# A two-layer gated block with routed experts: one group's results stored by block and fetched by token, the last two blocks added by matrix products, and a new order

## The chip, the cores and the metric

The kernel runs on one core of a Trainium2 chip. Its engines work beside each other, each through its own list of instructions in order: TensorE (PE: matrix products; PEld is its weight load), VectorE (DVE), ScalarE (ACT), GpSimd (POOL) and SyncE (SP, which only issues transfers here). They are held together by semaphores. Transfers between the chip's memory and the on-chip buffers run on 16 DMA engines, issued by SP, ACT or POOL. The metric is the device time of one execution in microseconds; less is better.

## The reference

The input x is 4 batches of 512 tokens of 128 numbers. Two layers follow each other; each is an attention over 77 context rows and a mixture of experts:

```python
x = x + tanh(g_xattn[l]) * attention_l(layernorm(x), ctx)      # 16 heads of 8
x = x + tanh(g_ffn[l])   * experts_l(layernorm(x))             # top 2 of 8 experts
# experts: softmax over 8 logits, the best two; each h = gelu(x @ w1[e] + b1[e]) (512 wide),
#          y = h @ w2[e] + b2[e]; the token gets p1 * y1 + p2 * y2
```

The second layer's attention adds a bias by position and a mask. All is float32.

## The kernel before, in words

**Attention.** A batch keeps its 512 tokens as 4 tiles of 128. Per layer and batch the steps are: statistics (`LS`), normalisation on ACT (`LT`), transposes (`LU`), query (`Q`), four score groups whose maxima DVE takes (`S`), lowering the query by the maxima (`M`, `W`), four exponent groups on PE and ACT (`X`), their sums with the values (`U`), the ratio (`E`, `T`, `N`) and the output product added to x (`F`). In layer 2 `S` and `X` also multiply a turned copy of the mask, tile `mt` (line 833, two buffers), into the products. The copy is made by `mask` on POOL, stored to memory, and loaded again by `mturn` (line 835).

**Routing.** The batches form two groups: 0 and 1, 2 and 3. For each token `Routing` finds the best two experts and the token's place in each expert's region of a table in memory, `xgs[group]`. `send` (line 525) gives the row numbers. `scatter` (line 538) sends the normalised rows there with indirect DMAs, one for 128 rows, all from POOL (line 419); each is preceded by a memset of a spare tile (line 418). A row carries 130 numbers: 128 of the token, its probability, and the row where its result belongs. `table` and `registers` turn the counts into 16 blocks a group, 7 of 256 rows and 9 of 128, whose first rows SP reads from registers.

**Experts.** Each block loads its expert's weights (`w`, line 623, 5 buffers) and its rows (`x`, line 631), transposes them (`t`), multiplies up (`u`, line 658; GELU on ACT, line 664), and down (`d`, line 673). DVE then adds the bias, multiplies by the probability (lines 681, 687) and makes the row numbers of the results (line 692). `y` scatters the block's results to `yks[layer][group]`, again by indirect DMAs of 128 rows from POOL. When a group's blocks are all scattered, `CL` loads each token's two results (line 711) and `CA` adds them to x (line 718), on POOL in layer 1, on DVE in layer 2, where the sum is also stored as output.

**Order.** The order of all steps is written out by hand in one long string, `ORDER`, of words such as `0y13.1`: layer 0, step y, block 13, group 1 (for attention and routing the last number is the batch). Every engine and every queue takes its own instructions in the order of these words. PE's matmul results go through six rotating PSUM banks.

Of the kernel before, what the change touches and what calls it, by code (L numbers as in the profile page):

```python
# [39 lines left out]
ROWS = SPARE + 2 * CAP  # L40


@with_exitstack
def flamingo_kernel(ctx: ExitStack, tc: tile.TileContext, a: dict, out: bass.AP):
# [53 lines left out]
    def load_mask(b):  # L98
        t = keep.tile([P, NT * KV + S], I32, tag="mi", name="mi", bufs=2)
        nc.sync.dma_start(out=t, in_=a["masks"][b])  # L100
        msk_i[b] = t
# [307 lines left out]

    class Scatters:  # L410


        def __init__(self):
            self.sent = []

# [11 lines left out]
    class Routing:  # L427


        def __init__(self, l, group):  # L430
            self.l, self.group = l, group
            self.carry = None
            self.left = {}
            self.scatters = Scatters()
# [47 lines left out]
        def choose(self):  # L482

            sm = self.sm
            self.pick = sm("pick", (P, 2, NT, E))
# [40 lines left out]
        def send(self, b):  # L526
# [8 lines left out]
            with nc.allow_low_precision(reason="one whole number and zeros"):  # L535
                nc.vector.tensor_reduce(to, v, AX.X, ALU.add)
            self.left[b] = self.chosen, to

        def scatter(self, b, t):
            rows, to = self.left[b]  # L540
# [3 lines left out]
        def table(self):  # L544
# [41 lines left out]
            nc.vector.scalar_tensor_tensor(hit[:, MARKS // 2 * E :], tail, block_no, row, ALU.is_equal, ALU.mult)  # L586
            begin = sm("begin", (P, 1))
# [13 lines left out]
    class Blocks:  # L601


        def __init__(self, routing):
            self.r, self.l, self.group = routing, routing.l, routing.group
            self.w, self.x, self.xT, self.h, self.y = {}, {}, {}, {}, {}
# [61 lines left out]
        def down(self, i):  # L668
            n, w, h, x = self.size(i), self.w.pop(i), self.h.pop(i), self.x.pop(i)
# [19 lines left out]
            )  # L689

# [3 lines left out]

        def scatter(self, i):
            yb, to = self.y.pop(i)
            for s in range(self.size(i)):
                self.scatters.send(yks[self.l][self.group], yb[:, s, :], to[:, s : s + 1])

    class Combine:  # L700


        def __init__(self, l, b):
            self.l, self.b = l, b

# [9 lines left out]
        def add(self):  # L715
# [3 lines left out]
            if self.l == 1:  # L719
                (nc.scalar if self.b == B - 1 else nc.sync).dma_start(out=out[self.b].rearrange("(p t) d -> p t d", p=P), in_=x)  # L720
# [11 lines left out]
    def routing_constants():  # L732
# [25 lines left out]
        return rank, region, below, ones, upper, mark, nth, block_no, row_of, pair_at, spare  # L758
# [3 lines left out]
    fill = const.tile([P, CAP // P * PAY], F32, tag="fill", name="fill")  # L762
# [4 lines left out]

    def clear(g, q):
        xg = xgs[g]
        for e in range(4 * q, 4 * q + 4, 2):  # L770
            nc.sync.dma_start(
                out=xg[e * REGION : (e + 2) * REGION, :].rearrange("(r q) d -> r (q d)", r=2)[:, : CAP * PAY].rearrange(
                    "r (p f) -> p r f", p=P
                ),
                in_=fill.unsqueeze(1).to_broadcast([P, 2, CAP // P * PAY]),
            )
        if q == 0:
            nc.sync.dma_start(
                out=xg[UNUSED : UNUSED + 256, :].rearrange("(p r) d -> p (r d)", p=P), in_=fill[:, : 2 * PAY]
            )  # L780

# [63 lines left out]
    def part(l, name, n):  # L845
        k, i = name[0], name[1:]
        A, R = at[l][n], routings[l][n // 2]
        if i.isdigit():
            i = int(i)
            if k in "wxtudy":  # L850
                G = blocks[l][n]
                {"w": G.load_w, "x": G.load_x, "t": G.turn, "u": G.up, "d": G.down, "y": G.scatter}[k](i)
            else:
                {"S": A.scores, "X": A.exps, "U": A.sums, "E": A.sums_out, "T": A.ratio, "Z": lambda t: R.scatter(n, t)}[k](i)
        elif name == "RS":
            R.stats(n)
        elif k == "R":
            {"T": R.turn, "U": R.turned, "L": R.logits, "C": R.choose, "D": R.choose_second, "M": R.count, "N": R.places, "X": lambda: R.send(n), "G": R.registers, "B": R.table}[i]()
# [8 lines left out]
        vclear0 pads0 ldx0 ones0 hot1 ldwv ldctx slots hot2 0LS.0 ldo0 ldgates ldq0 vclear2 gate keys0 vclear1 ldx1  # L867
        ldx2 hot5 ones1 ldx3 0LT.0 0LS.1 ldpos ldmask1 values1 0LS.2 values0 hot0 0LU.0 fill values2 second 0Q.0 0LT.1
        0S3.0 0LT.2 hot4 0S2.0 cleara1 0S0.0 cleara0 0LU.1 ldmask0 0LU.2 0S1.0 mask1 0Q.1 0M.0 0W.0 0S3.1 0Q.2 0LS.3
        0S2.1 0X0.0 0S0.1 0X1.0 0S1.1 pads1 0U0.0 0X2.0 0M.1 0U1.0 0E0.0 clearb0 0W.1 0X3.0 routing 0U2.0 0X0.1 0U3.0  # L870
# [132 lines left out]
```

## Time and profile before

| what | value |
|---|---|
| median of 3 runs | 428.34 us (427.59 to 429.42) |
| the profiled execution: its own time | 429.68 us |
| the profiled execution: its span | 427.6 us |
| mean granted PE clock | 0.966 |
| indirect DMAs: layer inputs, results | 64, 92 |
| one indirect DMA on POOL, its memset | 974 ns, 514 ns |
| moved by DMA | 77.91 MB, mean 182 GB/s |

The span runs from the first to the last instruction; the execution's own time has some 2 us around it. The page's second section cuts the span into 40 slices of 10.7 us; a digit is the busy share in tenths, and PEclk the clock that was granted to PE, in tenths. A group line names the line of the program, engine, operation, output and inputs, then how often it ran, busy time in all, the mean in ns, and the idle time before it. A timeline line gives start and length in us, then the instruction, and in brackets how long the engine had stood idle and what ended that. A line that begins with two times and a colon sums a stretch: the busy time of PE, PEld, DVE, ACT and POOL with instruction counts, then the clock, the DMA share and GB/s.

### The profile page before, as it was taken

To read this page: it belongs to the slowest core of one execution; us is meant where nothing else is said; L and a number is where in the kernel's file an instruction comes from. 1 tells how busy PE (TensorE), PEld (TensorE's weight loads), DVE (VectorE), ACT (ScalarE), POOL (GpSimd) and SP (SyncE) were. 2 spreads that over 40 slices of the span, in tenths; PEclk is the share of its full clock that TensorE was granted. 3 is DMA by queue.
4 is the path that set the end of the run, shared out by engine and by line. 5 is a ranking of instruction groups with operands and counts; after the bars stand their busy time and mean duration, and the time that the engine had idled before them with its cause. 6 is when DMAs were issued, how large, how long until landed. Compare 5 with 4: busy or idle time off the path is not lost.

```text
span 427.6 us, 9653 instructions
## 1 busy us (share of the span) xinstructions
PE 385.3 (90%) x3236; PEld 271.4 (63%) x3236; DVE 244.9 (57%) x931; ACT 225.0 (53%) x529; POOL 295.5 (69%) x478
## 2 busy tenths in 40 slices
PE   5999999987899999989999999999889999999850
PEld 2454545433789999987772355442669789988840
DVE  7786768864447634376774379684648233333342
ACT  2556776663374654447455965446564344435430
POOL 4743312887698989869986450987289898989860
PEclk9999999996699999999999999999989999999995
DMA  7396091112956799986514221014743776789855
GB/s 191 158 372 202 3 325 72 33 44 83 317 150 207 224 361 295 313 299 218 167 45 151 80 60 62 26 45 122 236 129 105 272 232 192 266 285 289 269 204 182
DMA packets 38977, 77.91 MB, mean 182 GB/s; under 512 B 6224, under 2 KB 22608, under 8 KB 38928
## 3 DMA queue, kind: packets, MB, share of 16 engines
q1 hardware_dynamic: 32640, 65.66, 47.9%
q0 software_dynamic: 4992, 10.30, 6.7%
q10 hardware_dynamic: 1296, 1.34, 0.9%
q8 instruction: 26, 0.43, 0.4%
q14 instruction: 23, 0.19, 0.1%
HBM read 55.47 MB, written 21.80 MB: 181 GB/s over the span
## 4 chain that ended last, share of the span: by engine, by line
PE 68%; DVE 12%; DMA 6%; POOL 5%; ACT 4%; issue 3%; SPq 0%; DVEq 0%; ACTq 0%; POOLq 0%
PE mm L673 16%; PE mm L658 15%; PE mm L353 8%; PE o L367 7%; PE mm L305 6%; POOL xg L419 3%; PE mm L279 3%; DVE mx L313 2%; PE mm L347 2%; ACT eT L359 2%; POOL apart L418 2%; PE mm L241 2%; PE mm L643 2%; PE mm L406 2%; DMA xb<-xg 1%
## 5 line engine op out<-in xcount | busy, mean ns | idle before, releaser
L664 ACT ACTIVATE h<-mm,w 128x128 f32<-128x128 f32 (+1 forms) x256 | 86.7, 415 | 99.3 <-issue 55.9
L419 POOL DMA_INDIRECT yk<-yb,to x92 | 89.6, 974 | 18.5 <-issue 12.2
L658 PE MATMUL mm<-xbT,w 128*128 128x128 f32 (+1 forms) x512 | 95.0, 331 | 6.6 <-DVE xbT L645 5.5
L673 PE MATMUL mm<-w,h 128*128 128x128 f32 x736 | 96.0, 281 | 0.7 <-ACT h L664 0.4
L673 PEld LDWEIGHTS mm<-w,h 128*128 128x128 f32 x736 | 89.2, 191 | 6.5 <-ACT h L664 3.6
L658 PEld LDWEIGHTS mm<-xbT,w 128*128 128x128 f32 x512 | 77.1, 194 | 15.0 <-DVE xbT L645 7.7
L418 POOL MEMSET apart<- 1x512 f32 x156 | 80.2, 514 | 0.1
L359 ACT ACTIVATE eT<-mm 77x512 f32<-77x512 f32 x128 | 65.4, 592 | 26.2 <-PE mm L353 25.7
L419 POOL DMA_INDIRECT xg<-rows,rows_to x64 | 62.8, 981 | 15.2 <-issue 13.0
L681 DVE TENSOR_TENSOR yb<-mm,w 128x128 f32<-128x128 f32 (+1 forms) x64 | 22.3, 348 | 67.2 <-PE mm L673 58.6
L313 DVE TENSOR_REDUCE mx<-mm 128x4 f32<-128x308 f32 x128 | 52.1, 469 | 11.5 <-PE mm L305 11.3
L353 PE MATMUL mm<-qa,kb 32*77 32x512 f32 x256 | 41.3, 617 | 0.5 <-DVE mx L313 0.5
L222 POOL TENSOR_SCALAR rstd<-mv 128x4 f32<-128x4 f32 x16 | 3.8, 236 | 54.2 <-DVE mv L220 40.9
L645 DVE COPY xbT<-mm 128x128 f32<-128x128 f32 (+1 forms) x64 | 21.7, 344 | 30.4 <-PE mm L643 30.4
L367 PE MATMUL o<-eT,vb 128*32 128x512 f32 x256 | 36.6, 631 | 0.0
L305 PE MATMUL mm<-kb,q 32*128 32x154 f32 x512 | 31.8, 322 | 0.8 <-DVE mx L313 0.5
L305 PEld LDWEIGHTS mm<-kb,q 32*128 32x128 f32 x512 | 22.6, 183 | 12.4 <-issue 3.1
L687 DVE TENSOR_TENSOR yb<-yb,xb 128x128 f32<-128x128 f32 (+1 forms) x64 | 24.1, 376 | 2.2
L643 PE MATMUL mm<-ident,xb 128*128 128x128 f32 x92 | 20.5, 281 | 1.2 <-DMA xb<-xg 1.2
L353 PEld LDWEIGHTS mm<-qa,kb 32*77 32x77 f32 x256 | 10.5, 140 | 13.4 <-issue 5.6
L223 POOL TENSOR_TENSOR rstd<-rstd,mhalf 128x4 f32<-128x4 f32 x16 | 16.7, 1044 | 1.3
L219 DVE BATCH_NORM_STATS2 st<-x 128x6 f32<-128x128 f32 x64 | 17.1, 267 | 0.2
(155 smaller groups left out, 445.6 us busy)
## 6 DMA issues: line engine op xcount, KB each, us to landing
w<-in_experts SPq DMA_DIRECT2D x64, 578.0 KB, 5.0
xg<-fill SPq DMA_DIRECT2D x8, 1040.0 KB, 6.0
xb<-xg SPq DMA_DIRECT2D x28, 130.0 KB, 3.6
y<-yk SPq DMA_DIRECT2D x14, 256.0 KB, 3.9
mt<-turns SPq DMA_DIRECT2D x4, 820.0 KB
xb<-xg SPq DMA_DIRECT2D x36, 65.0 KB, 4.4
mi<-in_masks SPq DMA_DIRECT2D x4, 410.0 KB
turns<-mb SPq DMA_DIRECT2D x8, 205.0 KB
```

The costliest lines, as they stand in the source:

```text
L305: nc.tensor.matmul(view[g][:, h], lhsT=self.q[h][rows, t * P : (t + 1) * P], rhs=kbs[l][rows, h, :, b, :], start=(l == 0), stop=(l == 0 or ...
L313: nc.vector.tensor_reduce(self.mx[:, t, :, 2 * g : 2 * g + 2], view[g], AX.X, ALU.max)
L353: nc.tensor.matmul(ps[g][:KV, :], lhsT=kbs[l][rows, h, w, b, :], rhs=self.qa[h][rows, :], start=(l == 0), stop=True,)
L359: nc.scalar.activation(self.eT[j][g][:KV, :], ps[g][:KV, :], AF.Exp)
L367: nc.tensor.matmul(self.o[a][g * 32 : (g + 1) * 32, :], lhsT=vbs[self.b][:, self.l, g, j, :], rhs=self.eT[j][g], start=(w == 0), stop=(w = ...
L418: nc.gpsimd.memset(apart, 0.0)
L419: i = nc.gpsimd.indirect_dma_start(out=to[:, :], out_offset=bass.IndirectOffsetOnAxis(ap=index, axis=0), in_=rows, in_offset=None)
L643: nc.tensor.transpose(ps[:, s * P : (s + 1) * P], x[:, s, :D], ident)
L658: nc.tensor.matmul(ps[:, g * 256 : g * 256 + n], lhsT=w[:, c * P : (c + 1) * P], rhs=xT[:, :n], start=True, stop=True,)
L664: nc.scalar.activation(h[:, c, :n], ps[:, g * 256 : g * 256 + n], AF.Gelu_apprx_tanh, bias=w[:, B1_AT + c : B1_AT + c + 1])
L673: nc.tensor.matmul(y[:, s * P : (s + 1) * P], lhsT=h[:, c, s * P : (s + 1) * P], rhs=w[:, W2_AT + c * P : W2_AT + (c + 1) * P], start=(c = ...
L687: nc.vector.tensor_tensor(yb[:, :n, :], yb[:, :n, :], x[:, :n, D : D + 1].to_broadcast([P, n, D]), ALU.mult)
```

## The change

1. **First layer, group 1.** A block's results are no longer scattered to their tokens' rows. SP stores each block as it is to a new table `yg`. `results` (new step `RP`, on DVE, per batch) works out in which row of `yg` each token's two results lie; for this `table` leaves three numbers per expert, and `send` keeps its row numbers as floats too. New steps `C0` to `C7` then fetch a batch's results, 128 rows each, by indirect DMAs from POOL, with the same memset ahead of each. They take the place of `CL` for batches 2 and 3.
2. **Second layer, group 1, last two blocks.** They are not scattered. `match` (step `o`) compares each row's target with the 512 token positions of a batch and makes a matrix of ones and zeros for both batches; `give` (called by `y`) multiplies it with the block's results and adds the product to x. `CL` and `CA` of batches 2 and 3 come before the last of these, with rows in memory that were cleared by the new step `cleary`, and the output is stored by `give` of block 15.
3. **Room.** The zero tile `fill` has 4 rows instead of 8 a partition, and clearing takes one DMA an expert instead of one for two; the integer mask `mi` has one buffer instead of two; `pick` has three.
4. **Order.** The whole string is laid out anew. Among much else, the turned masks are loaded for batches 1, 0, 2, 3 instead of 0, 1, 2, 3, and around the end of layer 1 it reads:

```
before: ... 0d12.1 0t15.1 1S2.1 0u14.1 1W.0 1S1.1 0d13.1 0u15.1 0y10.1 0y11.1 1X0.0 0y12.1 0d14.1 0y13.1 0y14.1
        0d15.1 1S3.1 0y15.1 1U0.0 1M.1 0CL.2 1X1.0 1X2.0 1U1.0 1W.1 1X3.0 1E0.0 1U2.0 0CL.3 mask2 0CA.2 1X0.1 1LS.2
        1U3.0 1E1.0 1X1.1 1LT.2 1U0.1 1T0.0 1X2.1 mturn2 1T1.0 1U1.1 1LU.2 0CA.3 1LS.3 1N.0 1X3.1 1F.0 1Q.2 ...
after:  ... 0u14.1 0u15.1 0d14.1 0y13.1 0d15.1 0y15.1 1S0.0 1M.0 0y14.1 0C0.2 0C7.2 1Q.1 0C1.2 1S1.1 1W.0 1S0.1
        0C0.3 1X0.0 1X1.0 1U0.0 1X2.0 0C6.2 1U1.0 1S3.1 1S2.1 ldmask3 0C4.2 0C2.3 0C7.3 0C2.2 1E0.0 1U2.0 0C5.2
        0C3.2 1M.1 1X3.0 0C6.3 1T0.0 1W.1 0C1.3 1X0.1 1U3.0 0C3.3 1E1.0 0CA.2 0C4.3 1LS.2 1X1.1 1T1.0 1U0.1 0C5.3
        1LT.2 1N.0 1X2.1 1LU.2 0CA.3 1F.0 1RS.0 1LS.3 1U1.1 1E0.1 1X3.1 mturn2 1T0.1 1Q.2 1S0.2 1U2.1 ...
```

The end of layer 2 reads in the new order:

```
... 1y12.1 1t14.1 1d13.1 1y13.1 1t15.1 1o14.1 1CL.1 1u14.1 1d14.1 1CA.1 1u15.1 1CL.2 1CL.3 1d15.1 1y14.1 1o15.1 1CA.2 1CA.3 1y15.1
```

The core of the diff:

```diff
+        def fetch(self, to, rows, index):
+            nc.gpsimd.memset(apart, 0.0)
+            nc.gpsimd.indirect_dma_start(
+                out=to, out_offset=None, in_=rows[:, :], in_offset=bass.IndirectOffsetOnAxis(ap=index, axis=0)
+            )
...
+        def results(self, b):
+            for k in range(3):
+                nc.vector.tensor_tensor(v[:, k], pick, self.of[:, k].unsqueeze(1).to_broadcast([P, 2 * NT, E]), ALU.mult)
+            nc.vector.tensor_reduce(r, v, AX.X, ALU.add)
...
+        def match(self, i):
+            for b in range(2):
+                nc.vector.tensor_scalar(oh[:, b], token_at, tok[:, b : b + 1], None, ALU.is_equal)
...
+        def give(self, i):
+            for b in range(2):
+                ps = bank()
+                for t in range(NT):
+                    own = slice(t * P, (t + 1) * P)
+                    nc.tensor.matmul(ps[:, own], lhsT=oh[:, b, own], rhs=yb[:, 0, :], start=True, stop=True)
+                x = x_sb[2 + b]
+                nc.vector.tensor_tensor(x, x, ps.rearrange("p (t d) -> p t d", d=D), ALU.add)
+                if i == NBLK - 1:
+                    (nc.scalar if b else nc.sync).dma_start(out=out[2 + b].rearrange("(p t) d -> p t d", p=P), in_=x)
...
         def scatter(self, i):
+            if self.last(i):
+                self.give(i)
+                return
             yb, to = self.y.pop(i)
+            if to is None:
+                nc.sync.dma_start(
+                    out=yg[self.at(i) : self.at(i) + n * P, :].rearrange("(s p) d -> p s d", p=P), in_=yb[:, :n, :]
+                )
+                return
```

## The prediction

> **What bounds the kernel now.** I read the page's engine and slice rows first, then the busy time by 10 us stretches, then the timeline around the three places that the change touches.
>
> ```profile
> PE 385.3 (90%) x3236; PEld 271.4 (63%) x3236; DVE 244.9 (57%) x931; ACT 225.0 (53%) x529; POOL 295.5 (69%) x478
> PE   5999999987899999989999999999889999999850
> PEclk9999999996699999999999999999989999999995
> L419 POOL DMA_INDIRECT yk<-yb,to x92 | 89.6, 974 | 18.5 <-issue 12.2
> L418 POOL MEMSET apart<- 1x512 f32 x156 | 80.2, 514 | 0.1
> ```
>
> PE is the bound nearly everywhere: 42.3 of 427.6 us idle, about 14 of it at the end. POOL is behind it: each indirect DMA costs 0.974 + 0.514 + a 0.17 gap = 1.64 us.
>
> ```profile
> 100.00:110.00 10.00, 8.07 (x43) 4.58 (x42) 6.11 (x29) 1.29 (x3) 5.95 (x11) 0.67 0.57 159
> 110.00:120.00 10.00, 9.70 (x48) 8.25 (x47) 4.14 (x15) 6.19 (x13) 7.82 (x11) 0.74 0.85 291
> 210.00:220.00 10.00, 10.00 (x145) 7.72 (x144) 8.58 (x26) 3.69 (x11) 8.98 (x14) 1.00 0.13 42
> 250.00:260.00 10.00, 9.07 (x146) 5.80 (x143) 8.78 (x27) 5.21 (x12) 1.78 (x3) 1.00 0.42 131
> ```
>
> Columns: length; busy PE, weight load, DVE, ACT, POOL; granted clock; DMA share; GB/s. From 120 to 250 PE is full (idle 2.5 us in 130), so nothing that only relieves POOL there can shorten the run. From 250 to 300 it idles 2.5 us. In the second layer's experts POOL is gapless too: its row over 311.3 to 410.5 counts 60 indirect DMAs, and 60 x 1.64 = 98.4 of 99.2 us.
>
> The handover of batch 2 to the second layer:
>
> ```profile
> 221.78 2.05 PE L673 MATMUL mm<-w,h 128*128 128x128 f32 x16
> 225.59 0.96 POOL L419 DMA_INDIRECT yk<-yb,to  x1 [0.17 <-issue]
> 230.74 2.63 POOL L718 TENSOR_TENSOR x<-x,y 128x512 f32<-128x512 f32 x2 [1.16 <-DMA y<-yk]
> 235.62 1.04 POOL L223 TENSOR_TENSOR rstd<-rstd,mhalf 128x4 f32<-128x4 f32 x1
> 240.84 1.65 ACT L233 ACTIVATE xn<-x,nmr,rstd 128x128 f32<-128x128 f32 x4
> 243.46 0.66 PE L241 MATMUL mm<-ident,xn 128*128 128x128 f32 x4
> 248.67 0.35 PE L295 MATMUL mm<-mt,ident 32*32 32x308 bf16 x16
> ```
>
> The last expert block leaves PE at 223.83. Batch 2's sum is ready at 233.37, its normalisation could start at 236.9 and starts at 240.84: some 4 us of slack. And the end:
>
> ```profile
> 412.30 1.26 PE L673 MATMUL mm<-w,h 128*128 128x128 f32 x8
> 414.56 1.16 POOL L419 DMA_INDIRECT yk<-yb,to  x1 [0.73 <-DVE to L692]
> 417.11 0.82 ACTq L711 DMA_DIRECT2D y<-yk  x2
> 422.16 2.02 DVE L718 TENSOR_TENSOR x<-x,y 128x512 f32<-128x512 f32 x3 [0.67 <-DMA y<-yk]
> 424.21 0.34 ACTq L720 DMA_DIRECT2D out<-x  x1
> ```
>
> PE ends at 413.56; scatter, load, sums and store take 14.0 us more.
>
> **Part 1, first layer, group 1.** Out: 23 scatters (37.7 us of POOL) and the four loads of batches 2 and 3. In: 16 direct stores on SP and 16 gathers (26.2 us of POOL). While PE is full the relief is worth only the stall that POOL's sums and their DVE slowdown caused at 191.80 (1.1 us). The cost is position: the scatters ran beside the blocks, and a gather can start only when the last block is stored. Call T the end of the last block's matmuls.
> Results written T+0.65 (DVE 0.29 + 0.29 and gaps). Stores issued by T+1.05, landed T+3.6: no row has a direct store of 65 KB alone; between 1.4 (end of the last scatter at 415.72 to the load that it released at 417.11) and 4.4 (median 65 KB load), I take 2.5. Then POOL, in its new order, does 14 gathers before batch 2's sum: 13 x 1.64 + 0.97 = 22.3, to T+25.9. No gather is in the trace; nearest is the scatter of the same 128 rows of 512 B. Its DMA part could be 0.6 to 1.2 us, 14 times; I take the row, 0.97. Sum 2.63: T+28.7. Statistics 1.75, rstd 1.35 (after one more gather, hidden by the statistics), shift 0.2, normalise 1.65, transposes: T+33.9.
> PE arrives at those transposes earlier. Moved behind T are four score groups (1.32 each), a query (1.9), a lowering (0.6) and one exponent group (1.6): 9.4 us, so T falls about 9.4 us earlier. I walked PE, DVE (1.63 per score group) and ACT (2.04 per exponent group) in the new order: PE gets there at T+28.8. Stall 4.5 us.
>
> **Part 2, the turned masks.** The two buffers of mt are now filled for batch 1, then batch 0, so batch 2's copy overwrites batch 1's and must wait for batch 1's last exponents. In the new order only 0.7 us of transposes and 1.9 us of query stand between those and batch 2's first scores. The copy at 235.32 moved data until about 239.6, 4.3 us: stall about 1.8 (nothing if other waits are later, 3 on a busy queue). Queued behind it on PE are the sums that would have filled it. First scores of batch 2: T+42.1. Before, 248.67 is T+24.8 by the old T, T+34.2 by the new, 34.9 with the transposes that now come first: 7.2 us later. PE's idle 2.5 us from 250 to 300 is all that can give it back; I take 1.5.
>
> **The clock.** Idle PE costs twice. After 94.9 PE stood for 2.49 us, then 0.68 twice with little work, and the two rows above lost 10 x (0.33 + 0.26) = 5.9 us of full clock. [...]
>
> **Part 3, the last two blocks.** Out: two scatters and their wait; batches 2 and 3 are loaded after the 60th indirect DMA instead of the 62nd. In, per block: 16 matmuls at 0.112 = 1.8 us of PE, three tiny and two 128x512 comparisons on DVE, two 128x512 sums from PSUM (0.75 each, as at line 408). A comparison is not in the trace: between 0.35 and 0.69 us (the tensor sum of that size), I take 0.5. Two paths. POOL's: last send ends 410.4, lands 411.9, loads 4.4, four sums 2.8, two last sums 1.5, store 3.4 (424.21 to 427.6): 424.0. DVE's: PE end 413.56, second-last block's sums to 416.2, comparisons to 417.8, four sums to 420.6, last two to 422.2, store: 425.6. The one gains 3.6, the other 2.0; I take 2.7.
>
> **Part 4, what is costed at nothing.** DVE: eight 8-column copies (0.17 to 0.3), 16 small operations in the results (about 4 us for both batches) and 5 in the table (1 us), against 18 operations of 0.15 to 0.23 that go; DVE is under 60% busy beside the experts, and 1 us on the path if it is not. The 16 stores wait on SP for a block's product with weight and row loads queued behind; those wait for the same blocks to free their buffers (48.9 us of SP waits), so nothing; uncovered, 1 to 2 us of PE per late weight. Clears: 18 DMAs instead of 10, and a new 1 MB one, some 0.45 us of SP each, ahead of masks and batch 3's rows, which are not needed until 30 us. One mask input buffer: each load waits for the POOL pass before it, early enough in the order. New order of the start: x of batch 0 meets as many DVE memsets, and its normalisation waited for ACT's key copies to 11.77 anyway: 0, give or take 1. The stretch of 88 to 110: output product moved ahead of a sum, its ACT copy uncovered instead: 0, give or take 2. The experts' order in layer 2: POOL still has 60 sends in a row, so 0, give or take 2.
>
> **Sum.** +7.2 +1.7 -1.5 -1.1 -2.7 = +3.6 us. The profiled execution's span is 427.6 and its own time 429.68, 2.1 around it and 1.3 above the median of the runs; applied to the median 428.34 this gives 431.9.
>
> **Rivals.**
> *Gathers hidden (faster).* If batch 2's sum is ready by T+23.8, PE never waits at its transposes. It decides at a gather of 1.29 us with its memset (a DMA part of 0.62) or if PE needs 34 us rather than 29 for the stretch without losing them elsewhere. Then -1.1 and -2.7 stand alone: 424.5. For: the new order puts three of batch 3's gathers ahead of batch 2's sum, which makes sense only where there is slack, and relieving POOL is real. Against: 1.64 us has held in 156 of 156 indirect DMAs.
> *Even.* The stalls come, but at full clock, with all 2.5 given back and the tail at 3.6: 428.34 + 7.2 - 1.1 - 2.5 - 3.6 = 428.3.
> *Clock falls as at 97 (slower still).* 5.9 instead of 1.7 and the tail at 2.0: 428.34 + 7.2 + 5.9 - 1.5 - 1.1 - 2.0 = 436.8.
>
> **Numbers.** About 0.5% (2.1 us) is what a measurement of this kernel can tell from no change. Chances: forecast 0.43, clock 0.10, even 0.15, hidden 0.32; so slower 0.53, same 0.15, faster 0.32. The forecast's own range is 430 to 435. The range for 8 in 10 reaches to the hidden case with 1 us for the costs at nothing, 423.5, and above to the clock's case, 437.5.
>
> **What would show it.** A PE gap of 3 to 6 us before batch 2's transposes, with POOL gapless in gathers before it; a gap of 1 to 2 us before batch 2's first scores, released by the mask copy; a clock under 1.00 in that stretch; 10 to 12 us between PE's last expert matmul and the end. Wrong if gathers take under 1.3 us each, if the second layer's batches 0 and 1 keep PE busy until batch 2 is there, or if the sends of the second layer's experts start earlier in relation to batch 2's arrival than before.

## The result, and the profile after

The kernel after takes 440.09 us (median of 4 runs, 439.49 to 440.48) against 428.88 us (427.59 to 431.71) for the kernel before beside it: ratio 1.024, 95% interval 1.020 to 1.028. That is 11 us slower. The forecast was 431.9 with a range up to 437.5: the direction was right, the size was not.

The first rows of the page after, as those of before were shown:

```profile
PE 395.3 (90%) x3268; PEld 276.9 (63%) x3268; DVE 251.1 (57%) x956; ACT 224.4 (51%) x529; POOL 282.8 (64%) x461
PE   6999999977999979999999798999889969999891
L430 POOL DMA_INDIRECT yk<-yb,to x67 | 65.2, 973 | 14.6 <-issue 9.6
L423 POOL DMA_INDIRECT y<-yg,res_at x16 | 15.6, 973 | 23.7 <-DMA yg<-yb 21.2
```

POOL has 12.7 us less to do, as intended. A fetch costs the 973 ns of a scatter, as assumed. But PE counts 10.0 us more busy time, and only some 4 of it are the 32 products with ones (3.97). Most of the rest is hidden waiting: the kernel multiplies nothing else anew, and a wait can count as busy (the same 12 mask products count 0.42 us in one group and 1.61 in the next, below). Some 4 us of it are located below, in the attention groups.

Busy time of the engines in stretches of 10 us (columns: length; PE, weight load, DVE, ACT, POOL; clock; DMA share; GB/s), first the kernel before, then the kernel after:

```profile
150.00:160.00 10.00, 9.62 (x84) 9.14 (x82) 3.92 (x17) 5.70 (x20) 8.95 (x13) 1.00 1.02 371
240.00:250.00 10.00, 9.98 (x110) 4.75 (x108) 5.33 (x21) 8.68 (x18) 4.70 (x5) 1.00 0.00 0
350.00:360.00 10.00, 9.99 (x69) 9.02 (x68) 2.99 (x10) 4.47 (x12) 8.89 (x13) 1.00 0.74 250
...
150.00:160.00 10.00, 6.95 (x51) 6.11 (x50) 3.37 (x14) 4.35 (x16) 8.99 (x13) 1.00 0.98 346
240.00:250.00 10.00, 7.95 (x72) 2.62 (x68) 4.47 (x16) 6.60 (x13) 8.93 (x13) 1.00 0.38 115
350.00:360.00 10.00, 5.65 (x43) 4.85 (x43) 3.53 (x15) 2.17 (x8) 8.99 (x13) 1.00 0.77 220
```

PE loses 2.7, 2.0 and 4.3 us in these three. They are: the first block of group 1 among layer 1's experts, the handover, and the same block in layer 2. The handover in the timeline after (start, length, instruction, idle time before it and what ended it):

```profile
217.14 1.95 PE L713 MATMUL mm<-w,h 128*128 128x128 f32 x16
...
222.77 1.13 POOL L423 DMA_INDIRECT y<-yg,res_at  x1 [21.23 <-DMA yg<-yb]
...
245.04 2.63 POOL L808 TENSOR_TENSOR x<-x,y 128x512 f32<-128x512 f32 x2
247.70 0.29 DVE L220 BATCH_NORM_STATS2 st<-x 128x6 f32<-128x128 f32 x1 [4.66 <-POOL x L808]
...
250.24 0.63 PE L398 MATMUL mm<-ident,on 128*128 128x128 f32 x4 [2.08 <-DVE on L388]
...
252.18 1.03 PE L242 MATMUL mm<-ident,xn 128*128 128x128 f32 x4
...
259.11 0.56 PE L296 MATMUL mm<-mt,ident 32*32 32x308 bf16 x16
```

The last expert block ends at T = 219.09. The first fetch starts at T+3.7, the sum of batch 2 is done at T+28.6, its transposes run from T+33.1 and its first scores from T+40.0. The wait is where the forecast put it, in POOL's row of 14 fetches, but it reaches PE by another way: DVE stands in order behind batch 2's statistics for 4.66 us, and the normalisation of batch 0 that is queued behind them (`on`, line 388) comes late for PE. And the end:

```profile
421.49 0.97 POOL L430 DMA_INDIRECT yk<-yb,to  x1 [0.44 <-DVE tok L745]
...
424.06 1.26 PE L713 MATMUL mm<-w,h 128*128 128x128 f32 x8
...
426.22 0.34 SPq L810 DMA_DIRECT2D out<-x  x1
...
426.67 1.04 SPq L801 DMA_DIRECT2D y<-yk  x2
...
434.88 0.34 SPq L765 DMA_DIRECT2D out<-x  x1
```

The last send ends at 422.46, but the loads of batches 2 and 3 go at 426.67, behind the store of batch 1 on SP, and at 426.22 on ACT, when the sum of batch 1 (done at 426.20) has freed a tile. From PE's last expert product to the end it takes 13.3 us, against 14.0 before.

By stages, in us from the start of each profile. A second pair, c_before and c_after, is the two kernels unchanged on another chip (last in the experiments):

| stage | before | after | change | second pair |
|---|---|---|---|---|
| end T of layer 1's experts | 223.83 | 219.09 | -4.7 | -5.4 |
| T to first scores of batch 2 | 24.84 | 40.02 | +15.2 | +14.4 |
| to the first send of layer 2's experts | 62.73 | 62.39 | -0.3 | -0.2 |
| to the last expert product | 102.16 | 103.82 | +1.7 | +0.7 |
| to the end | 14.04 | 13.28 | -0.8 | -0.8 |
| span | 427.6 | 438.6 | +11.0 | +8.6 |

So nearly all of the loss is there when batch 2's first scores begin: 10.4 us in the first pair (259.11 against 248.67), 9.0 in the second.

### The profile page after: what moved, and what is told of

It reads as the page before. It is cut to its first block, busy times and chain, and to the rows that moved or that the text cites. A ratio compares the mean times of both kernels' runs of the same rounds, so it can differ in the third digit from the quotient of the medians.

```text
span 438.6 us, 9739 instructions
## 1 busy us (share of the span) xinstructions
PE 395.3 (90%) x3268; PEld 276.9 (63%) x3268; DVE 251.1 (57%) x956; ACT 224.4 (51%) x529; POOL 282.8 (64%) x461
## 4 chain that ended last, share of the span: by engine, by line
PE 45%; POOL 21%; DMA 12%; DVE 10%; issue 6%; ACT 4%; SPq 1%; ACTq 0%; DVEq 0%; POOLq 0%
PE mm L698 8%; PE mm L713 7%; PE mm L354 7%; PE mm L306 5%; POOL apart L429 5%; POOL xg L430 5%; PE o L368 4%; POOL yk L430 4%; DMA y<-yk 3%; POOL y L423 3%; PE mm L280 3%; DMA w<-in_experts 2%; DMA xb<-xg 2%; DMA xg<-rows,rows_to 2%; PE mm L407 2%
## 5 line engine op out<-in xcount | busy, mean ns | idle before, releaser
L713 PEld LDWEIGHTS mm<-w,h 128*128 128x128 f32 x736 | 90.2, 193 | 4.6 <-ACT h L704 3.0
L430 POOL DMA_INDIRECT yk<-yb,to x67 | 65.2, 973 | 14.6 <-issue 9.6
L429 POOL MEMSET apart<- 1x512 f32 x131 | 67.4, 515 | 0.1
L721 DVE TENSOR_TENSOR yb<-mm,w 128x256 f32<-128x256 f32 (+1 forms) x64 | 22.3, 349 | 73.2 <-PE mm L713 70.3
L423 POOL DMA_INDIRECT y<-yg,res_at x16 | 15.6, 973 | 23.7 <-DMA yg<-yb 21.2
L727 DVE TENSOR_TENSOR yb<-yb,xb 128x256 f32<-128x256 f32 (+1 forms) x64 | 24.8, 388 | 2.2
L220 DVE BATCH_NORM_STATS2 st<-x 128x6 f32<-128x128 f32 x64 | 17.1, 267 | 5.8 <-POOL x L808 5.6
L683 PEld LDWEIGHTS mm<-ident,xb 128*128 128x128 f32 x92 | 12.5, 148 | 10.3 <-DMA xb<-xg 5.1
```

What stands on the lines that cost most here:

```text
L423: nc.gpsimd.indirect_dma_start(out=to, out_offset=None, in_=rows[:, :], in_offset=bass.IndirectOffsetOnAxis(ap=index, axis=0))
L429: nc.gpsimd.memset(apart, 0.0)
L430: i = nc.gpsimd.indirect_dma_start(out=to[:, :], out_offset=bass.IndirectOffsetOnAxis(ap=index, axis=0), in_=rows, in_offset=None)
L683: nc.tensor.transpose(ps[:, s * P : (s + 1) * P], x[:, s, :D], ident)
L713: nc.tensor.matmul(y[:, s * P : (s + 1) * P], lhsT=h[:, c, s * P : (s + 1) * P], rhs=w[:, W2_AT + c * P : W2_AT + (c + 1) * P], start=(c = ...
```

## The experiments

Each ratio is against the kernel before on the same chip, with its 95% interval. The kernel after has 1.024. Word moves are shown as diffs of the string `ORDER`.

### One half of the change without the other, and two first suspects

**e_rg.** In the new order SP comes to the register read of group 1 later and stood there until 145 and 349 us. The words are put back to their old places:

```diff
-0d5.0 0u6.0 0w9.0 0Z1.3 0t7.0 0x10.0 0u7.0 0RP.3 hot3 0t8.0 0Z2.3 0RG.3 0w10.0
+0d5.0 0w9.0 0x10.0 0RG.3 0u6.0 0Z1.3 0t7.0 0u7.0 0RP.3 hot3 0t8.0 0Z2.3 0w10.0
...
-1t6.0 1d5.0 ... 1w10.0 1RG.3 1x8.0 1d6.0 1x9.0
+1t6.0 1x8.0 1x9.0 1d5.0 1RG.3 ... 1w10.0 1d6.0
```

> The kernel after, with seven words of its order moved and nothing else: the registers of group 1 (RG.3) are read where the order before reads them, right behind the down product of block 5, with the loads of weights 9 and rows 10 (layer 1) and of rows 8 and 9 (layer 2) ahead of them. Theory A: in the order after, SP stands at the register read until about 145 us in layer 1 and until 349 us in layer 2, with the next blocks' loads queued behind it, and PE runs out of rows at 141 to 158 and 347 to 359. Then the span falls by 6 to 8.5 us against the kernel after (431 to 434 us) and PE is full again in both stretches. Rival B: the whole loss is the handover (gathers, masks, clock): then this changes the time by less than 1.5 us.

Measured 1.0245 (1.020 to 1.029): nothing. PE still has 7.95 and 5.45 us in 150 to 160 and 350 to 360. Theory A falls. SP's wait for the register only took the place of its wait for free row and weight buffers, in the same queue.

**e_gather.** Batch 2's fetches ahead of batch 3's:

```diff
-0C0.2 0C7.2 ... 0C0.3 ... 0C6.2 ... 0C4.2 0C2.3 0C7.3 0C2.2 ... 0C5.2 0C3.2 ... 0C6.3 ... 0C1.3 ... 0C3.3 ... 0CA.2 0C4.3 1LS.2
+0C0.2 0C1.2 0C2.2 0C3.2 0C4.2 0C5.2 0C6.2 0C7.2 0C0.3 ... 0CA.2 0C1.3 1LS.2 0C2.3 ... 0C7.3
```

> The kernel after with the 16 fetches in another order and nothing else: batch 2's eight first, then one of batch 3's, then batch 2's sums and its statistics, then batch 3's other seven. Theory A: the sum of batch 2 starts after 9 instead of 14 fetches, 5 x 1.63 = 8.2 us sooner, so batch 2's transposes no longer wait and the stall of some 5 us at the handover goes: 3.5 to 5 us faster than the kernel after (435 to 436.5 us), less what the wait costs when batch 3 comes later. Rival B: the loss at the handover is PE work in another place, not the wait for the fetches: within 1 us of the kernel after.

Measured 1.0315 (1.025 to 1.038), not faster. The wait at batch 2 goes (first scores at T+37.6 instead of T+40.0) and comes back one batch later. DVE now stands behind the statistics of batch 3, and PE behind DVE:

```profile
257.01 0.29 DVE L220 BATCH_NORM_STATS2 st<-x 128x6 f32<-128x128 f32 x1 [4.90 <-POOL x L808]
...
259.46 0.45 PE L296 MATMUL mm<-mt,ident 32*32 32x308 bf16 x4 [4.92 <-DVE on L388]
```

**e_order.** The new order with the old means:

```diff
-        return l == 0 and group == 1
+        return False
-LAST = 2
+LAST = 0
-0y14.1 0C0.2 0C7.2 ...
+0y14.1 0CL.2 0CL.3 ...
```

> The new order with the old means: group 1 of layer 1 scattered to its tokens and loaded (CL.2 and CL.3 where the fetches began), the last two blocks of layer 2 scattered, their output stored by the sums, no step for the row numbers, no clearing of result rows. Theory A: the loss lies in the order (late register read, 7 to 8 us in both layers) and, for the rest, in the fetches' place. Then this kernel is 6 to 10 us slower than the kernel before (435 to 439 us), with the same two empty stretches of PE at 141 to 158 and 347 to 359. Rival B: the loss comes from the new means alone: within 2 us of the kernel before (426 to 431 us).

Measured 1.051 (1.046 to 1.055), worse than either theory. With 23 scatters more on POOL, its sums of batches 0 and 1 come late, DVE waits 11.7 us for them, and PE 10.6 us at 203.86. So the new order needs POOL's relief; in the old one the same scatters cost little (the stall of 1.1 us at 191.8).

**e_means.** The old order with the new means:

```diff
-0CL.2 ... mask2 0CA.2 1LS.2 ... 0CL.3
+mask2 0C0.2 ... 0C7.2 0CA.2 1LS.2 0C0.3 ... 0C7.3
```

> The old order with the new means: group 1 of layer 1 stored by block and fetched by token, the fetches where the loads of batches 2 and 3 were (batch 2's eight first, then its sum, then batch 3's eight after its statistics), the last two blocks of layer 2 by products with ones and the new tail; the integer mask keeps two buffers and the choice tile has two. Theory A (the order carries the loss): the register read keeps its early place, so it lacks the 7 to 8 us; the first transposes of batch 2 wait for nine fetches instead of fourteen; in all 426 to 432 us. Rival B (the means carry the loss): 436 to 441 us.

Measured 1.052 (1.048 to 1.055), again worse than either theory. Three waits of PE stand out: 4.45 us for rows at 208.0 (T is 232.0), 3.60 us at batch 2's transposes (255.3), and 8.00 us at 273.0, since batch 3's fetches start only behind batch 2's sum. Why the rows are late at 208.0 is not shown: the stores now stand ahead of row loads on SP, but from 185 to 210 SP waits only 1.9 us at a store and 11.3 us for free weight tiles. Each half of the change alone is worse than both together, so neither alone names the cause.

### How much is the fetches

**e_half.** Half of them, and **e_gather_ls**, the order of e_gather with batch 3's statistics later:

```diff
-            for k in range(2):
+            for k in range(1 if fetched(self.l, self.b // 2) else 2):
...
-0CA.3 1F.0 1RS.0 1LS.3 1U1.1 ... 1RU.0 1LT.3
+0CA.3 1F.0 1RS.0 1U1.1 ... 1RU.0 1LS.3 1LT.3
```

> The kernel after, but only four of the eight fetches of batches 2 and 3 are made (each token gets only the result of its first choice from layer 1; the second choice's is left out of x). So POOL has 8 x 1.63 = 13 us and two sums of 1.3 us less to do between the last expert block of layer 1 and the second layer's work on batches 2 and 3. Theory A: the handover sets when POOL can begin the sends of layer 2, and from there it works without a gap for 101 us to the end: the first send moves from 321.5 to some 314 to 316 and the end moves by as much, 5.5 to 7.5 us faster than the kernel after (ratio to the kernel before about 1.008 to 1.012). Rival B: the sends of layer 2 are set by PE and by the loads of that stretch: under 2 us faster than the kernel after.

> The kernel after with batch 2's fetches first, as in the last run of that kind, and one word more moved: batch 3's statistics stand right ahead of its normalisation, five steps later, so VectorE does not stand in order behind them while the reciprocals of batch 1 wait. Theory A: the 4.9 us wait of PE for those reciprocals goes, batch 2's scores come at some 34 us behind the last expert block instead of 40, and the kernel is 3 to 6 us faster than the kernel after, if batch 3 is not late in turn. Rival B: the fetches as a whole are too slow, and the wait moves on to batch 3's transposes: within 2 us of the kernel after.

e_half measured 1.014 (1.007 to 1.021): between the theories, nearer to A. Its first send comes 4.3 us sooner (317.2), but 1.7 of them are there at T already. e_gather_ls measured 1.028 (1.024 to 1.032): rival B. The wait moved once more, to 3.5 us ahead of a product of batch 1, behind DVE's routing steps, which stand behind the same statistics. These two and e_none (below), where PE waits for no fetch at batch 2, show its first scores at the same place:

| kernel | T | first scores of batch 2 | first send of layer 2 |
|---|---|---|---|
| after | 219.09 | T+40.02 | 321.50 |
| e_gather_ls | 217.98 | T+37.33 | 322.04 |
| e_half | 217.44 | T+37.34 | 317.18 |
| e_none | 218.98 | T+37.35 | 319.17 |
| e_back | 227.18 | T+42.91 | 333.87 |
| e_half_back | 226.89 | T+31.04 | 321.63 |

The wait for fetches is 40.02 - 37.34 = 2.7 us, and taking it away still leaves T+37.3.

**e_none** (run later, with the attention runs) has no fetch at all:

> The kernel after without any fetch and without the sums of batches 2 and 3 behind layer 1 (their layer 1 experts' results are left out). Theory A: what is left of the loss is the order of the attention steps and not the fetches, so this is at most 1.5 us faster than with half of the fetches: ratio 1.010 to 1.014, with score and exponent groups still at 1.43 and 1.78 us. Rival B: all of the loss is the fetches: 1.000 to 1.005.

Measured 1.018 (1.013 to 1.023). So 1.8 of 2.4% are there without a single fetch, by the intervals at least half of the loss; and this kernel leaves out the sums of batches 2 and 3 as well, which the kernel before has. Rival B, that all is the fetches, falls. Theory A's figure for the size (1.010 to 1.014) was too low; its second half, that the attention groups stay as long, held (23.7 and 29.3 us, below).

**e_half_back** and **e_back.** The moved attention steps go back between the expert blocks, with half and with all of the fetches:

```diff
-0y9.1 0u12.1 0u13.1 ... 0t14.1 ... 0t15.1 ... 0u14.1 0u15.1 ... 0y15.1 1S0.0 1M.0 ... 1Q.1 0C1.2 1S1.1 1W.0 1S0.1 0C0.3 1X0.0 ... 1S3.1 1S2.1
+0y9.1 1S0.0 1M.0 0u12.1 1Q.1 0u13.1 ... 0t14.1 1S0.1 ... 0t15.1 1S2.1 ... 0u14.1 1W.0 1S1.1 0u15.1 1X0.0 ... 0y15.1
```

> The kernel after with half of the fetches (the results of the second choice in layer 1 are left out for batches 2 and 3), as before, and with the attention steps that the new order moved behind the last expert block of layer 1 (three score groups, a query, a lowering, an exponent group; a fourth score group stays) put back between the expert blocks. Theory A: the same steps cost more when they stand in a row, where each waits for VectorE's maxima and ScalarE's exponents, than between expert products: then the first send of layer 2 comes 2 to 4 us sooner than with half of the fetches alone (313 to 315 instead of 317.2) and the time is within 1% of the kernel before. Rival B: what is left of the loss is in the expert blocks of both layers: within 1 us of the kernel with half of the fetches.

> The kernel after with all of its fetches and the same attention steps put back between the expert blocks. Theory A: these steps covered the fetches; the last expert block of layer 1 ends some 7 us later, the fetches start as much later, and the wait for batches 2 and 3 grows: 2 to 6 us slower than the kernel after. Rival B: the fetches' wait costs less than the steps in a row: equal to the kernel after or faster by up to 3 us.

Measured 1.021 (1.015 to 1.027) and 1.050 (1.043 to 1.058). The first goes against its theory A: not faster than e_half (1.014), with 3.7 us of PE waiting behind fetches at one place. In the second PE waits 14.75 us at one place (theory A's direction, a size beyond it). The moved steps are the fetches' cover: without them the wait is not 2.7 but 14.8 us. (All four score groups went back, not three: seven stand before T again, as in the kernel before.) And they cost about the same in either place of the new string: T comes 9.5 us later than in e_half, and from T to the first scores, without that wait of 3.7, it takes 10.0 us less. So that they stand behind T is not what costs.

### The tail

**e_ones.** The kernel before with the ones alone (`LAST = 2`, `fetched` false) and the tail:

```diff
-1t14.1 1CL.0 1u14.1 1t15.1 1y12.1 1d14.1 1CL.1 1y13.1 1u15.1 1y14.1 1d15.1 1CA.0 1CA.1 1y15.1 1CL.2 1CL.3 1CA.2 1CA.3
+1t14.1 1u14.1 1t15.1 1y12.1 1o14.1 1CL.0 1CL.1 1d14.1 1y13.1 1u15.1 1CA.0 1CA.1 1CL.2 1CL.3 1d15.1 1y14.1 1o15.1 1CA.2 1CA.3 1y15.1
```

> The kernel before with only the last two blocks of layer 2 changed: they are not scattered but added by products with ones, the rows that they would have filled are cleared early, batches 0 and 1 are loaded and added ahead of the last block's product, and batches 2 and 3 right behind the last send. Theory A (as forecast): two sends less in POOL's gapless row, 1 to 4 us faster than the kernel before. Rival B: the comparisons, sums and the wait for the load are as long as what they replace, within 1 us.

Measured 1.000 (0.998 to 1.003): rival B. The loads of batches 2 and 3 do not go when the last send has ended:

```profile
412.28 1.07 POOL L430 DMA_INDIRECT yk<-yb,to  x1 [0.17 <-DVE tok L746]
...
415.11 3.23 SPq L810 DMA_DIRECT2D out<-x  x2
...
418.00 0.86 ACTq L801 DMA_DIRECT2D y<-yk  x2
418.50 0.83 SPq L801 DMA_DIRECT2D y<-yk  x2
```

The last send ends at 413.35, the loads start at 418.0 and 418.5. They need the two `y` tiles that batches 0 and 1 hold until DVE has added them (417.97), and one queue stands at their stores. Two sends fewer end a wait that another follows by as much.

**e_tail**, **e_ones2**, **e_ones4.** Batches 0 and 1 earlier, in the kernel after and in e_ones; then four blocks by ones (with the words for it, not shown):

```diff
 e_tail
-1t13.1 1CL.0 1d12.1 ... 1w15.1 1y9.1 1CA.0 ... 1o14.1 1CL.1 1u14.1 1d14.1 1CA.1 1u15.1 1CL.2 1CL.3 1d15.1 1y14.1
+1t13.1 1d12.1 ... 1w15.1 1CL.0 1CL.1 1y9.1 ... 1o14.1 1u14.1 1CA.0 1CA.1 1d14.1 1CL.2 1CL.3 1u15.1 1y14.1 1d15.1
 e_ones2
-1o14.1 1CL.0 1CL.1 1d14.1 1y13.1 1u15.1 1CA.0 1CA.1 1CL.2 1CL.3 1d15.1
+1CL.0 1CL.1 1u13.1 ... 1y12.1 1CA.0 1o14.1 1d14.1 1y13.1 1CA.1 1CL.2 1CL.3 1u15.1 1d15.1
 e_ones4
-LAST = 2
+LAST = 4
```

> The kernel after with its last 30 words laid out otherwise and nothing else: batches 0 and 1 are loaded behind the last weight and row loads instead of ahead of them, both are added and stored before the last block's up product, so that the loads of batches 2 and 3 have free buffers and a free queue and can go when the last send has landed (423.9 us in the kernel after, where they went at 426.2 and 426.7). Theory A: 2 to 3.5 us faster than the kernel after. Rival B: VectorE's comparisons and sums behind the last product are the longer path: under 1 us.

> The kernel before with the last two blocks of layer 2 added by products with ones, as in the earlier run of that part alone, but with its last 23 words laid out otherwise: batches 0 and 1 are loaded right behind the last weight load and added and stored one block sooner, so that the loads of batches 2 and 3 go when the last send has landed; in the earlier run they went at 418.5, 3.7 us behind that landing, because SP stood at the two output stores. Theory A (the part's gain was lost in SP's order): 2 to 4 us faster than the kernel before. Rival B (VectorE's comparisons and sums behind the last product set the end): within 1.5 us of it.

> As the last one, but the last four blocks of layer 2 are added by products with ones: 58 instead of 60 indirect DMAs in POOL's gapless row of layer 2, 2 x 16 matmuls and their comparisons and sums more on PE and VectorE. Theory A (POOL's row of sends sets the end of layer 2): 2 x 1.64 = 3.3 us faster than with two blocks. Rival B (PE is as near to its bound there as POOL): 0 to 1.5 us slower than with two blocks, for 2 x 1.95 us of PE and 2 x 2.2 us of VectorE.

Measured 1.022 (1.017 to 1.027), 1.010 (1.006 to 1.014) and 1.011 (1.006 to 1.017): no gain that can be told from none, and two losses. A reason lies in the edit of these runs itself. ACT issues the loads of batch 3, and in these orders the issue stands ahead of the GELU of block 15. It waits for a free `y` tile, and so do the GELU and PE behind it, as in e_ones2:

```profile
422.78 1.14 ACT L704 ACTIVATE h<-mm,w 128x128 f32<-128x128 f32 x4 [7.00 <-DVE x L808]
423.20 2.08 PE L713 MATMUL mm<-w,h 128*128 128x128 f32 x8 [5.98 <-ACT h L704]
```

So these three do not tell their theories apart; a tail with the gain of the forecast was not found. With 58 sends instead of 60 (e_ones4) the last send ends 3.6 us sooner than in e_ones2 (412.12 against 415.72) and the time is the same: behind that wait of ACT, POOL's row does not set the end.

### The longer attention groups

A score group of layer 2 is 16 mask products, 16 products and DVE's maxima; an exponent group 12 and 8 products and ACT's exponentials. Summed over the layer, each from its first product to the start of what follows on PE or the wait before that (the short listed waits inside a group are in it, 0.6 us in the kernel before, 1.7 in the kernel after):

| kernels | 16 score groups | 16 exponent groups |
|---|---|---|
| before, c_before, e_ones | 20.3, 20.6, 20.3 us | 26.8, 27.5, 26.8 us |
| after, c_after, e_tail | 23.2, 24.0, 23.2 us | 29.3, 29.3, 29.3 us |
| e_half, e_none, e_order | 23.2, 23.7, 23.8 us | 29.3, 29.3, 29.6 us |
| e_half_back, e_back | 23.0, 23.1 us | 29.4, 29.8 us |

5 us more in every kernel with the new string, 4.2 of them not listed as a wait: also where the means are old (e_order), where no fetch runs (e_none), and where the moved steps stand between the expert blocks again. What it is can be seen in the kernel after:

```profile
238.84 0.42 PE L348 MATMUL mm<-mt,ident 32*32 32x512 bf16 x12
...
240.36 2.04 ACT L360 ACTIVATE eT<-mm 77x512 f32<-77x512 f32 x4 [4.09 <-PE mm L354]
...
241.24 1.61 PE L348 MATMUL mm<-mt,ident 32*32 32x512 bf16 x12
...
241.97 0.10 PEld L348 LDWEIGHTS <-ident 32*32 32x32 bf16 x3 [0.39 <-issue]
242.46 0.09 PEld L348 LDWEIGHTS <-ident 32*32 32x32 bf16 x2 [0.39 <-issue]
```

The 12 mask products of one exponent group take 0.42 us at 238.84. The next group's take 1.61, with pauses in steps of ACT's exponentials (2.04 us for four): each group takes four of the six PSUM banks, and this one follows the other with only a transposition and a lowering between. The trace's semaphore records agree: each three of these products (one bank's) wait for ACT's semaphore, which rises at 240.96, 241.45, 241.93 and 242.41, and the last three sets start at 241.49, 241.97 and 242.45. So PE waits here for ACT to free bank after bank. That the other long groups of the layer wait in the same way is not shown one by one, and no run has more banks.

**e_attn**, **e_half_attn**, **e_rev.** The attention steps of layer 2 in the other kernel's relative order, in the same slots:

```diff
 e_attn, e_half_attn (after)
-1Q.1 0C1.2 1S1.1 1W.0 1S0.1 0C0.3 1X0.0 1X1.0 1U0.0 1X2.0 0C6.2 1U1.0 1S3.1 1S2.1 ...
+1Q.1 0C1.2 1S0.1 1S2.1 1W.0 0C0.3 1S1.1 1X0.0 1S3.1 1U0.0 0C6.2 1M.1 1X1.0 1X2.0 ...
 e_rev (before)
-1S0.2 1RT.0 mturn3 1U2.1 1E0.1 1LT.3 1S2.2 1S1.2 1U3.1 1S3.2 1E1.1 ...
+1S0.2 ... 1U2.1 ... 1S1.2 1U3.1 1E1.1 1S3.2 1S2.2 1RU.0 1LT.3 ...
```

> The kernel after with the attention steps of layer 2 behind the last expert block of layer 1 in the relative order that they have in the kernel before, in the same slots of the string; fetches, routing, expert blocks and all else stay where they are. In the new order a score group of layer 2 takes PE 1.43 us and an exponent group 1.78 us, in the old one 1.25 and 1.62 us, together 5.4 us over 16 groups of each, without a wait being listed. Theory A: this is the order of the attention steps, and 2 to 5 us of the kernel after's loss go: ratio to the kernel before 1.013 to 1.020. Rival B: the longer groups come from what is beside them (fetches, DVE's other work): ratio unchanged at 1.024.

> As the last one, with half of the fetches (the results of the second choice in layer 1 are left out for batches 2 and 3). Theory A: both costs add, the fetches' wait (4.3 us of the first send of layer 2) and the attention order (up to 5.4 us): ratio to the kernel before 1.002 to 1.008. Rival B: 1.014 as with half of the fetches alone.

> The kernel before with the attention steps of layer 2 from the query of batch 2 on in the relative order that they have in the kernel after, in the same slots, and nothing else. Theory A: about half of the longer groups come with it, 2 to 4 us slower than the kernel before (ratio 1.005 to 1.010). Rival B: no change (0.997 to 1.003).

Measured 1.036 (1.032 to 1.039), 1.025 (1.019 to 1.030) and 1.024 (1.021 to 1.026). Both theories of the first two fall: the old relative order makes the kernel after slower, with groups as long (22.7 and 30.7 us in e_attn), perhaps since in foreign slots the steps meet other neighbours. e_rev, beyond its theory A, shows only how much hangs on this: a reordering of the attention steps alone costs the kernel before 2.4%, as much as the whole change, here in listed waits (5.2 us for ACT's copies of `oT`, 2.3 for its query). Which neighbours make the groups of the new order long stays open.

### Is the loss in layer 1 real

**c_before**, **c_after.** Both kernels unchanged, one profile each on one chip.

> The kernel before, unchanged, for a second trace on the same chip as the next run. Theory A: the differences by stage that the first two traces show are the change's. Then the last expert block of layer 1 ends at 223 to 225 us, the first send of layer 2 starts at 311 to 313, and the score and exponent groups of layer 2 take 20.3 and 26.8 us. Rival B: the end of layer 1 scatters by 2 to 3 us between profiles of one program, as five profiles of kernels that equal the kernel after up to there did (216.3 to 219.1), and the 3.4 us that layer 1 seems to lose are mostly that.

> The kernel after, unchanged, on the same chip. Theory A: the last expert block of layer 1 ends 4.7 us sooner than in the kernel before on this chip, as in the first pair of traces (8.15 us of work having been moved behind it). Rival B: it ends 6 to 8 us sooner, so the expert blocks of layer 1 lose under 2 us and the first send of layer 2 is late by the fetches and the longer groups alone (23.2 and 29.3 us).

433.07 and 441.57 us. T is 225.75 and 220.32, 5.4 us apart: between the two theories, nearer to A. But T does scatter. Nine profiles of kernels with the new order up to there have it from 216.3 to 220.3 (mean 218.0), and the two used here are the latest of them; three with the old order have 222.3 to 225.8 (mean 223.9). By the means T fell by some 6.

The loss between 120 and 160 is no scatter. PE's busy time there is 35.8 to 37.2 us in all thirteen kernels with the new order of layer 1 (mean 36.6), and 38.3 to 39.3 in all seven with the old one (mean 39.0). It goes with the order and not with the means: e_order has 36.5, e_means 38.7.

## Why the prediction was wrong in size

In short: the fetches' place, which the forecast put first, costs what its row of fetches said or less. The steps that failed are three. The new order of layer 1's blocks was put at nothing, and costs some 2.4 us of T where PE waits for rows. Each attention group was walked with the length that it has alone, and the groups are 5 us longer together. And the tail was to give 2.7 us, because batches 2 and 3 would be loaded two sends sooner; they are not, and it gave 0.8.

**Right.** A fetch costs POOL what a scatter does; the first went at T+3.7 (forecast T+3.6), the sum of batch 2 was done at T+28.6 (T+28.7), its transposes ran from T+33.1 to T+34.1 (T+33.9). With that the rival of hidden fetches fell. PE came to stand at T+29.1 (T+28.8).

By the terms of the forecast's sum (first pair; second pair in brackets):

| term | forecast | measured |
|---|---|---|
| T, with the stall saved at 191.8 | -9.4 - 1.1 | -4.7 (-5.4) |
| T to first scores, stalls in it | +17.3 | +15.2 (+14.4) |
| clock | +1.7 | in the other terms |
| layer 2 after that, without 0.7 for transposes done sooner | -0.7 - 1.5 | +1.3 (+0.4) |
| tail | -2.7 | -0.8 (-0.8) |
| sum | +3.6 | +11.0 (+8.6) |

**T falls about 9.4 us, and a stall of 1.1 goes.** It fell by 4.7 and 5.4, by the means above by some 6. Moving the steps did what was forecast: with them put back (e_half_back, e_back) T is 226.9 and 227.2, some 9 us more than the mean of 218.0. But these two, with the steps in their old place, lie 3 us above the kernels with the old order (223.9), where the forecast has 1.1 below. So what fails is the rest of the new order of layer 1, which Part 4 costed at nothing. Two things nearly fill this gap of 4. The attention groups ahead of T are longer there too, by 1.5 (seven score groups take 8.96 us and the exponent group 1.81, in the kernel before 7.73 and 1.52; so the same steps were worth only 8.15 us in the kernel before). And 2.4 are the loss in 120 to 160, where PE waits for the rows of group 1's first block:

```profile
156.69 0.44 PE L683 MATMUL mm<-ident,xb 128*128 128x128 f32 x2 [1.68 <-DMA xb<-xg]
```

In the new order this block comes 13.4 us after PE's product for the blocks' first rows (143.28), in the old one 18.4. Why the load is late is not settled. The register read is not it (e_rg). Part 4 counted SP's 48.9 us of waits for weight tiles and passed over 43.1 us for row tiles on the same list; from 110 to 215 us SP waits 24.7 us for row tiles in the kernel after, 15.6 in the kernel before. And the DMA engines, full in 150 to 160 in both kernels (0.98 and 1.02), were busy only 0.60 in the 10 us before that, against 0.84. No run changed the number of row tiles.

**Stalls of 4.5 and 1.8, clock 1.7.** The wait for the fetches was 2.1 us where it is listed, 2.7 in all by the comparison with e_half and e_none. The mask copy cost nothing, since the step "batch 2's copy overwrites batch 1's" was wrong:

```profile
239.34 0.37 SPq L933 DMA_DIRECT2D mt<-turns  x1
```

SP issued it right after the last mask products of batch 0 (238.84 and 0.42 long), while batch 1's were still to come. No run shows the clock's 1.7 for this wait, and the clock cost nothing either: in the kernel after it stayed at 1.00 through the gap of 2.08 us and on to 412.49. Behind gaps of 3.7 to 14.75 us in other runs it stood at 0.5 for 3.4 to 17.1 us (last section). (Of the gaps that the forecast named for the clock, the trace has 2.49 and 0.68 us; the third is 1.43 us, at 107.45.) Forecast 8.0, measured 2.7.

**T to first scores.** That this term came close (17.3 against 15.2) is two errors against each other. The stalls in it were 3.6 us too large. Without them the forecast had first scores at T+35.8, and a PE that waits for no fetch takes 37.3 (e_none): the steps were 1.5 too small. Between T and the first scores the kernel after spends 5.3 us more on score groups than the kernel before, 3.2 on exponent groups, 1.9 on the query and 0.5 on lowering: 10.9, where 9.4 was taken. The walk gave each group its own length and saw no price for two that follow each other on four of six banks each.

**1.5 given back.** Nothing was; 1.3 and 0.4 us came on top. This is not batches 2 and 3 in longer groups. Their groups are 1.9 and 2.3 us longer (their score groups take 12.5 us from 259 on, 10.8 in the kernel before from 248.6 on), but the stage that holds them, up to the first send, is 0.3 and 0.2 us shorter. The excess lies behind it, between the first send and the last expert product (+1.7 and +0.7), where PE has the empty stretch at 350 to 360. What makes that stretch was not settled.

**Part 3, -2.7.** Measured -0.8 in the tail, and 0 for the part alone in the kernel before (e_ones). The step that failed is "batches 2 and 3 are loaded after the 60th indirect DMA": they are loaded when the sums of batches 0 and 1 free their two tiles and the queue is past their stores, 4 to 5 us after that DMA. No run has a tail without a wait of this kind, so what the part would then give stays open.

**What the 11 us are.** By the runs: 2.7 for the fetches, 2.4 in the order of layer 1's blocks, about 3 in the attention groups of batches 0 and 1 (3.5 and 2.8 us longer), 1.7 or 0.7 in layer 2's experts, -0.8 in the tail; the rest is not located. The two pairs differ by 2.4 us in the span and T scatters by 4, so no finer split is claimed. The mechanism that the forecast put first, the fetches' place, is there and is the smaller part; e_none without it is still 1.8% slower.

## What to carry to other kernels

A step that is moved off a relieved engine onto the handover has to be covered there by other work, and that cover has a price too: steps that were cheap in one order can wait for each other's banks in another (0.42 and 1.61 us for the same 12 products here), and the profile counts much of that as busy. A wait that is removed pays only up to the next one on the same step, so list all that a transfer waits for (source, free tile, its queue, the issuing engine's order) before counting a gain. In an order written by hand, half of a change tells little of the whole: both halves alone were worse than both together. And one profile places a stage only to within its scatter (4 us for T here); a count over all kernels that share the order settled what the pair could not.

## What the runs showed of the hardware

In these profiles the granted clock fell behind some gaps of PE and stayed down for a time. By the clock records it fell to 0.5 between 2.1 and 5.1 us after these gaps began, sometimes when PE was back at work: 2.1 in e_back (gap of 14.75 us), 2.5 in e_gather (4.92), 3.0 in e_order (10.6), 4.4 in e_half_back (3.7), 5.1 in e_means (4.45 and 8.0). It came back 3.8 to 7.9 us after PE's restart. A gap of 2.08 us (the kernel after, PE back at 250.24) left it at 1.00, but in the same profile one of 1.67 us (PE back at 412.18) was followed by 3.42 us at 0.5 from 412.49; in the kernel before one of 2.49 us at 94.9, with little work behind it, was followed by 6.83 us at 0.5 from 98.13. So the length of the gap alone does not tell whether the clock falls. The stretches at 0.5 in these runs that end with PE at work last 3.4, 6.8, 13.7 or 17.1 us, close to one, two, four and five times the shortest. Why it falls when it does, and why for these lengths, is not shown.

In all nine kernels with 147 indirect DMAs (after, c_after, e_rg, e_gather, e_gather_ls, e_means, e_tail, e_back, e_attn) POOL pauses once for 1.7 us in layer 2 (1.71 us until 366.79 in the kernel after, 1.70 until 368.71 in c_after), ahead of the same instruction of its list, the 395th. Neither e_half with 139 nor the kernel before with 156 has it. What it is stays open.
